# The last 96 features of a float32 gate and up stage: seven products on sums of x for eight on sums of weights

## The chip, the cores and the metric

One core of a Trainium2 chip runs the whole program, in one launch. The metric is device microseconds of that core: the median of the runs shown. One further execution is profiled; it has its own time, and the span of its trace (from the first to the last instruction of the program) is a little shorter than that time. Engines are named as in the profile: PE multiplies matrices, PEld is the loading of its stationary operand, DVE and ACT work on vectors, POOL and SP issue transfers (DMAs), and "PSUM banks" hold PE's results, 128 partitions by 512 float32 each.

## The reference, cut to what matters

One transformer layer in float32 on x of 2 x 2048 tokens by 512: attention over the feature axis, then a feed-forward part whose weights are looked up in a table of 16 values.

```python
x = x + attention(layernorm(x), Wq, Wk, Wv, Wo)
n = layernorm(x)                          # 4096 tokens x 512
gate = n @ lut[gate_idx].T                # 512 -> 1376
up   = n @ lut[up_idx].T                  # 512 -> 1376
x = x + (silu(gate) * up) @ lut[down_idx].T   # 1376 -> 512
```

1376 features are ten blocks of 128 (f = 0 to 9) and a last one of 96 (f = 10). This last block is what the change is about.

## The kernel before

**Stages in order.** Gram matrices of the normalized x (to 77 us), small 512 x 512 products for the attention (to 160), its product with the tokens and the second norm (to 276), gate and up for f = 0 to 9 (to 736.87), gate and up for the last 96 features (to 778.93), and the product with the down weights (to the end, 1052).

**Tiling of gate and up.** The tokens are 8 chunks of 512 (c), taken in four pairs (p). For a feature block f and a pair p a unit (class GateUp) computes four results, gate and up for chunk 2p and for chunk 2p + 1, with the contracted 512 split in two halves of 256. That is a 2 x 2 by 2 x 2 product of blocks, and a unit needs seven block products for it instead of eight, on sums of blocks that are made beforehand: of the weights (S1, S2, S3, S4, by of_both in pair_job, L390, four DVE operations for each f) and of the tokens (T1, T2, T3, T4, by f_sums, in rooms of the pool keep). In the units f = 0 to 9 the weights are stationary (128 x 128, one feature block) and 512 tokens are the moving operand. Each block product is two matmuls of 512 columns into one PSUM bank (mm, L1219). The seven are called a1, c1, a2, c2, b, a3, a4, by the bank they go to; a, c and b are the banks. Products on the same bank follow each other: a2 adds on top of a1 after ACT has copied a1 out, and so on. For f of 2 and above, a second level of the same scheme works on pairs of feature blocks and pairs of p, with banks x, z and w; for it, the operands of the odd p were changed in place (in the products with 21, T4 and 22 the first half stands for a difference).

**Order of the work.** The order on PE, ACT, DVE and SP is written by hand: what the program issues first comes first on its engine. Line.run (L1397) issues the seven products of a unit and, between them, what remains of the unit before: its a4 after the new unit's c1, its Silu (end, L1384) and its product gate x up (out, L1387) still later. between() (L1537) runs after each product: it takes one operation from the list todo, and then fills DVE with steps of the lookup of weights (step, L465; fill, L474) up to a lead over PE that a small clock model (Clock) estimates. The lookup makes all gate, up and down weights from their indices on DVE. Its jobs come in a fixed order; the jobs of the down weights for blocks 0 to 5 store to DRAM (wdd), and wd_load brings these six back into SBUF.

**The last 96 features** (class LastRows, L1452) go another way. Here x is stationary, 128 tokens at a time, and the moving operand is 192 columns, gate and up side by side. ACT copies the looked up weights into one tile side by side (copied, L1465, before the unit f = 9, p = 3), and DVE makes six sums and negatives of them (weights, L1470). For each chunk c, each of four token blocks j takes four matmuls of 192 columns, over the four blocks of 128 of the contracted 512 (products, L1501): 8 x 4 x 4 = 128 matmuls. That is all eight block products; the sums of weights are there only because xs holds some sums of tokens in place of the tokens. Two token blocks share a bank; the banks x, z, w and b take turns. ACT applies Silu to the gate half and DVE multiplies it with the up half (rows, L1516), straight from PSUM, and after the second half of a chunk SP stores 128 x 384 to hrd.

The loop at L1841 goes over the eight chunks and two halves (n = 0 to 15). line.flush (L1443) ends the last unit of f = 9 behind the first four token products. Into the list todo go, in this order: the sums of the weights, wd_load(0) into room sq1 (its load is issued on SP at once, at L1827) with eight DVE sums, the turning back of the norms; wd_load(1) into room a3 when the lookup of blocks 4 and 5 has been issued; sums of the hidden values for the first down unit at n = 8; and the loads of xn_back (ask_for_normed) at n = 12. Then come the units of the down stage (class Down), whose products have 256 columns and go to the banks a, c and b.

Products in LastRows, for one half of a chunk:

```python
for jj in range(2):
    j = 2 * h + jj
    for i, (x, w) in enumerate(pairs):       # four pairs
        nc.tensor.matmul(
            ps[:, jj, :], x[:, j * P : (j + 1) * P], w,
            start=i == 0, stop=i == len(pairs) - 1,
        )
```

Of the kernel before, what the change touches and what calls it, by code (L numbers as in the profile page):

```python
# [51 lines left out]
F32 = mybir.dt.float32  # L52
# [17 lines left out]
def tile_attn_ffn(  # L70
# [303 lines left out]
    def pair_job(f):  # L374
        f0, rows = FT[f]
        n = KB * rows
        made = []

        def dest():
            made.append(wgu.tile([P, 2, KB * P], F32, tag="w", name=f"w_{f}", bufs=4)[:, :, :n])  # L380
            return made[0]

        def after():
            for to, i in ((gw, 0), (uw, 1)):
                to[f] = made[0][:, i, :].rearrange("p (k r) -> p k r", k=KB)
            if f < NFT - 1:
                deferred.append((lambda: f < 3 + ended[0], of_both()))
            yield 0.1

        def of_both():  # L390
            g, u = gw[f], uw[f]
            t = wgu.tile([P, 3, 2, P], F32, tag="s", name=f"s_{f}", bufs=3)
            a11, a12, a21, a22 = g[:, 0:2, :], g[:, 2:4, :], u[:, 0:2, :], u[:, 2:4, :]
            s1, s2, s4 = (t[:, q, :, :rows] for q in range(3))
            for op, d, v, w in (
                (ALU.add, s1, a21, a22), (ALU.subtract, s2, s1, a11),
                (ALU.subtract, a21, a11, a21), (ALU.subtract, s4, a12, s2),
            ):
                nc.vector.tensor_tensor(d, v, w, op)
                yield 0.42  # L400
            gu[f] = {"11": a11, "12": a12, "S3": a21, "22": a22, "S1": s1, "S2": s2, "S4": s4}

        loads = [idx[:, KB * f0 : KB * f0 + n] for idx in (gate_idx, up_idx)]
        return Job(f"w{f}", P, n, loads, dest, after, lambda: f < 4 + ended[0])
# [813 lines left out]

    def mm(ps, pairs, first):  # L1219

        for i, (lhsT, rhs) in enumerate(pairs):
            clock.matmul(rhs.shape[-1])
            nc.tensor.matmul(  # L1223
                ps, lhsT, rhs, start=first and i == 0, stop=i == len(pairs) - 1,
                skip_group_check=not first,
            )
        clock.made(ps)

# [220 lines left out]
            self.last.out()  # L1449
            self.last = None  # L1450

    class LastRows:  # L1452

        TAGS = "xzwb"

        def __init__(self):
            self.w, self.v = (
                wgu.tile([P, 3, 2, P], F32, tag="s", name=f"last_{i}", bufs=3)  # L1460
                .rearrange("p a b c -> p (a b c)").rearrange("p (k r) -> p k r", k=KB)
                for i in range(2)
            )

        def copied(self):  # L1465
            f, r = NFT - 1, LAST
            nc.scalar.copy(self.w[:, :, :r], gw[f])
            nc.scalar.copy(self.w[:, :, r:], uw[f])

        def weights(self):  # L1470
            w, v = self.w, self.v
            u = wgu.tile([P, 2, KB * P], F32, tag="w", name="last_2", bufs=4)
            u = self.u = u.rearrange("p a e -> p (a e)")[:, : 2 * KB * LAST].rearrange(
                "p (k r) -> p k r", k=KB
            )
            minus = nc.vector.tensor_scalar_mul
            return [
                lambda: add(u[:, 0, :], w[:, 2, :], w[:, 3, :]),
                lambda: minus(u[:, 1, :], w[:, 2, :], -1.0),
                lambda: add(v[:, 0:2, :], w[:, 0:2, :], w[:, 2:4, :]),  # L1480
                lambda: minus(v[:, 2:4, :], w[:, 0:2, :], -1.0),
                lambda: add(u[:, 2, :], v[:, 0, :], v[:, 1, :]),
                lambda: minus(u[:, 3, :], v[:, 0, :], -1.0),
            ]

        def pairs(self, c):

            w, v, u, x = self.w, self.v, self.u, xs[c // 2]
            second = c // 2 % 2
            if c % 2 == 0:  # L1490
                one, two = (("11", w[:, 0:2, :]), ("21", w[:, 2:4, :], u[:, 0, :], u[:, 1, :]))
            else:
                one, two = (("T3", v[:, 2:4, :]), ("22", v[:, 0:2, :], u[:, 2, :], u[:, 3, :]))
            t = x[one[0]]
            out = [(t[:, kk, :], one[1][:, kk, :]) for kk in range(2)]
            t = x[two[0]]
            if second:
                return out + [(t[:, 1, :], two[2]), (t[:, 0, :], two[3])]
            return out + [(t[:, kk, :], two[1][:, kk, :]) for kk in range(2)]

        def products(self, c, h, n):  # L1501
            r = 2 * LAST
            ps = psum(self.TAGS[n % 4], f"rows_{c}_{h}")[:, : 2 * r]
            ps = ps.rearrange("p (j r) -> p j r", j=2)
            pairs = self.pairs(c)
            for jj in range(2):
                j = 2 * h + jj
                for i, (x, w) in enumerate(pairs):
                    clock.matmul(r)
                    nc.tensor.matmul(  # L1510
                        ps[:, jj, :], x[:, j * P : (j + 1) * P], w,
                        start=i == 0, stop=i == len(pairs) - 1,
                    )
            return ps

        def rows(self, c, h, ps):  # L1516
            if h == 0:
                t = ffn.tile([P, CH], F32, tag="u2", name=f"hrow_{c}", bufs=2)
                self.h = t[:, : J * LAST].rearrange("p (m j a) -> p m j a", m=M_LAST, j=J)
            g = ffn.tile([P, CH], F32, tag="h0", name=f"grow_{c}_{h}", bufs=2)  # L1520
            g = g[:, : 2 * LAST].rearrange("p (j r) -> p j r", j=2)
            nc.scalar.activation(g, ps[:, :, :LAST], AF.Silu)
            nc.vector.tensor_tensor(  # L1523
                self.h[:, :, 2 * h : 2 * h + 2, :].rearrange("p m j a -> p j m a"),
                g.rearrange("p j (m a) -> p j m a", a=Q),
                ps[:, :, LAST:].rearrange("p j (m a) -> p j m a", a=Q), ALU.mult,
            )
            if h:
                nc.sync.dma_start(hrd[c], self.h)

    sums_of = []
    to_load = []
# [251 lines left out]
    for (f, p), following in zip(units, units[1:] + [(NFT, 0)]):  # L1784
        while f not in gu or f > 1 and p and not all(o.ready(f | 1) for o in seconds):
            clock.dve += step()
        assert p in xs
        if (f, p) == (2, 0):
            sums_of += [(o, f) for o in seconds]
        if 2 < f < NFT - 2 and f % 2 and p == NPR - 1:  # L1790
            sums_of += [(o, f + 1) for o in seconds]
        while f % 2 == 0 and p and sums_of:
            next_sums_left()
        for op in to_load:
            op()
        to_load[:] = loads(*following)
        if (f, p) == (2, 1):
            todo += by_two(in_place)
        if (f, p) == (NFT - 2, NPR - 1):
            while uw.get(NFT - 1) is None:  # L1800
                step()
            last_rows = LastRows()
            last_rows.copied()
        u = GateUp(f, p)
        line.run(u)
        if p == NPR - 1:
            passed[0] = f + 1
        if (f, p) == (0, 3):
            xnp.release()
            x2p = tc.alloc_tile_pool(name="x2p", bufs=1, side="right", reuse_waits="tile")  # L1810
            for g in range(2):
                for o in seconds:
                    ops, last = o.sums(g)
                    todo += [one_by_one(op) for op in ops]
                    in_place.append(last)
# [6 lines left out]
    h = Hidden(0, 0)  # L1822

    def wd_load(q):
        tag, n = (("sq1", 4), ("a3", 2))[q]
        t = room(tag, f"wd_{tag}")
        nc.sync.dma_start(t[:, :n, :], wdd[:, 4 * q : 4 * q + n, :])  # L1827
        wd1.extend(t[:, i, :] for i in range(n))
# [5 lines left out]

        return by_two(down_sums(PARTS[0][2 * q : 2 * q + 2], place))

    while K1 - 4 not in done:
        step()
    todo += by_two(last_rows.weights()) + wd_load(0) + [lambda: [r.turn_back() for r in ln2]]
    n = 0  # L1840
    for c in (0, 4, 2, 6, 1, 5, 3, 7):  # L1841
        for half in range(2):
            ps = last_rows.products(c, half, n)
            if n == 0:
                line.flush()
            last_rows.rows(c, half, ps)
            between()
            n += 1
            if len(wd1) < K1 and (n == 6 or K1 - 2 in done):
                while K1 - 2 not in done:  # L1850
                    step()
                todo += wd_load(1)
            if n == 8:
                todo += by_two(h.sums())
            if n == 12:
                ask_for_normed(0, 0)
                ask_for_normed(0, 1)
    units = [Down(h, 0)]
    for op in todo:
        op()  # L1860
# [95 lines left out]
```

## Time and profile before

| What | Value |
|---|---|
| Median of 3 runs | 1053.54 us (1053.24 to 1054.12) |
| The profiled execution's own time | 1053.92 us |
| Its span | 1052.1 us |
| Mean granted PE clock | 0.999 |
| Gate and up, f = 0 to 9 | 276.00 to 736.87 us |
| Last 96 features | 736.87 to 778.93 us |
| Down stage | 778.93 to 1052 us |

How to read the profile: busy time is the time in which an engine executed something; of PE and PEld the durations of neighbouring instructions overlap, since matmuls are pipelined and a load runs beside the matmul ahead of it. Their ends are modelled; starts are what was recorded. A group of instructions is named by its line in the program, its engine and operation, the tile that it writes, and the tiles that it reads after an arrow. A name such as a_g is bank a of a gate and up unit, a_d that of a down unit, rows the banks of LastRows. "Idle before" is time in which an engine stood still ahead of an instruction, with what ended the wait. "128*128 128x192" means that 128 rows and 128 columns of the array are in use and that the result is 128 by 192.

### The profile page before, as it was taken

To read this page: it belongs to the slowest core of one execution; us is meant where nothing else is said; L and a number is where in the kernel's file an instruction comes from. 1 tells how busy PE (TensorE), PEld (TensorE's weight loads), DVE (VectorE), ACT (ScalarE), POOL (GpSimd) and SP (SyncE) were. 2 spreads that over 40 slices of the span, in tenths; PEclk is the share of its full clock that TensorE was granted. 3 is DMA by queue.
4 is the path that set the end of the run, shared out by engine and by line. 5 is a ranking of instruction groups with operands and counts; after the bars stand their busy time and mean duration, and the time that the engine had idled before them with its cause. 6 is when DMAs were issued, how large, how long until landed. Compare 5 with 4: busy or idle time off the path is not lost.

```text
span 1052.1 us, 11796 instructions
## 1 busy us (share of the span) xinstructions
PE 1044.1 (99%) x3746; PEld 697.3 (66%) x3746; DVE 832.2 (79%) x1558; ACT 397.1 (38%) x769; POOL 107.2 (10%) x160
## 2 busy tenths in 40 slices
PE   9999999999999999999999999999999999999998
PEld 5668888888544444444444444444998888888887
DVE  7888788888898788897898888889668888756644
ACT  4652531566732234434434434444222323211111
POOL 0000000001120210320131032014000000000000
PEclk9999999999999999999999999999999999999999
DMA  8750317268681465885696679569755766566773
GB/s 345 248 167 21 72 23 159 48 158 241 182 229 60 150 209 195 195 230 179 192 198 221 198 175 241 190 174 221 245 159 174 245 202 203 186 198 210 225 220 120
DMA packets 128429, 192.22 MB, mean 183 GB/s; under 512 B 18912, under 2 KB 59104, under 8 KB 127344
## 3 DMA queue, kind: packets, MB, share of 16 engines
q1 hardware_dynamic: 83696, 111.71, 33.4%
q0 software_dynamic: 15776, 39.92, 17.4%
q10 hardware_dynamic: 28896, 39.85, 11.5%
q8 instruction: 29, 0.48, 0.2%
q14 instruction: 32, 0.26, 0.1%
HBM read 110.17 MB, written 81.26 MB: 182 GB/s over the span
## 4 chain that ended last, share of the span: by engine, by line
PE 95%; DVE 2%; DMA 1%; issue 1%; ACT 1%; ACTq 0%; SPq 0%; DVEq 0%
PE a_g L1223 22%; PE a_d L1223 14%; PE y L914 9%; PE c_g L1223 9%; PE c_d L1223 7%; PE gp L542 6%; PE b_d L1223 4%; PE z_g L1223 4%; PE x_g L1223 4%; PE w_g L1223 3%; PE rows L1510 3%; PE b_g L1223 2%; PE ea_t L697 1%; PE ea_s L697 1%; PE ea_p L697 1%; PE ea_m L697 1%
## 5 line engine op out<-in xcount | busy, mean ns | idle before, releaser
L1223 PE MATMUL a_g<-xT_a,s 128*128 128x512 f32 x240 | 113.1, 594 | 0.0
L362 DVE COPY_PREDICATED w<-b_w,w 128x1024 f32<-128x1024 int16 (+1 forms) x77 | 98.6, 1280 | 1.3
L1223 PEld LDWEIGHTS a_g<-xT_a,s 128*128 128x128 f32 x240 | 45.2, 190 | 58.2 <-issue 54.5
L1223 PE MATMUL c_g<-xb,w 128*128 128x512 f32 x160 | 75.3, 593 | 0.9 <-DVE xb L172 0.9
L1223 PE MATMUL a_g<-xb,w 128*128 128x512 f32 x160 | 75.2, 592 | 0.0
L542 PE MATMUL gp<-xn_a 128*128 128x128 f32 (+3 forms) x256 | 69.8, 434 | 0.6 <-DVE xn_a L208 0.5
L350 DVE TENSOR_SCALAR w<-idx_w,lut_x,lut_sb 128x1024 int32<-128x1024 int32 (+1 forms) x88 | 67.9, 794 | 0.2
L1223 PE MATMUL a_d<-dT,hs_a 128*128 128x256 f32 x256 | 65.7, 378 | 0.0
L542 PEld LDWEIGHTS gp<-xn_a 128*128 128x128 f32 x256 | 43.8, 190 | 27.7 <-issue 15.1
L181 ACT COPY p_d<-a_d 128x256 f32<-128x256 f32 x32 | 11.9, 372 | 118.4 <-PE a_d L1223 114.0
L1223 PEld LDWEIGHTS c_g<-xb,w 128*128 128x128 f32 x160 | 30.3, 190 | 39.5 <-issue 36.6
L1223 PEld LDWEIGHTS a_g<-xb,w 128*128 128x128 f32 x160 | 30.4, 190 | 37.9 <-issue 35.2
L1223 PEld LDWEIGHTS a_d<-dT,hs_a 128*128 128x128 f32 x256 | 48.5, 189 | 6.8
L172 DVE TENSOR_TENSOR r<-r,p_d 128x256 f32<-128x256 f32 x64 | 27.1, 423 | 31.7 <-ACT p_d L181 23.4
L362 DVE COPY_PREDICATED wd<-b_wd,wd 128x1024 f32<-128x1024 int16 (+1 forms) x42 | 50.8, 1210 | 0.6
L914 PE MATMUL y<-m,nT 128*128 128x256 f32 x192 | 47.3, 381 | 1.2 <-ACT y L928 0.7
L181 ACT COPY u<-a_g 128x512 f32<-128x512 f32 x40 | 23.4, 586 | 58.1 <-PE a_g L1223 58.0
L172 DVE TENSOR_TENSOR r<-r,a_d 128x256 f32<-128x256 f32 x64 | 26.7, 418 | 20.4 <-PE a_d L1223 20.4
L1510 PEld LDWEIGHTS rows<-last,xb 128*128 128x128 f32 x256 | 41.6, 190 | 1.0 <-DVE hrow L1523 0.5
L1510 PE MATMUL rows<-last,xb 128*128 128x192 f32 x256 | 42.0, 326 | 0.2 <-DVE hrow L1523 0.2
L172 DVE TENSOR_TENSOR c<-a_g,p 128x512 f32<-128x512 f32 x40 | 27.6, 689 | 18.1 <-PE a_g L1223 17.0
L914 PEld LDWEIGHTS y<-m,nT 128*128 128x128 f32 x192 | 36.2, 190 | 7.2 <-ACT y L928 1.5
(368 smaller groups left out, 2228.8 us busy)
## 6 DMA issues: line engine op xcount, KB each, us to landing
hd<-h SPq DMA_DIRECT2D x80, 256.0 KB, 3.5
h<-hd SPq DMA_DIRECT2D x40, 512.0 KB, 6.1
nl<-nd SPq DMA_DIRECT2D x32, 256.0 KB, 5.7
xnd<-xn_f SPq DMA_DIRECT2D x16, 512.0 KB, 5.6
fl<-xnd POOLq DMA_DIRECT2D x32, 256.0 KB, 6.4
xn_back<-xnd SPq DMA_DIRECT2D x32, 256.0 KB, 3.7
rd<-r SPq DMA_DIRECT2D x32, 256.0 KB, 2.6
r<-rd SPq DMA_DIRECT2D x32, 256.0 KB, 3.5
```

The source lines that it names most:

```text
L172: nc.vector.tensor_tensor(dest, a, b, op)
L181: nc.scalar.copy(dest, a)
L350: vec.tensor_scalar(dest.bitcast(I32), idx, lut_x[:rows, k : k + 1], lut_i[:rows, at : at + 1], ALU.bitwise_and, ALU.bitwise_xor,)
L362: vec.copy_predicated(dest, masks[level - 1], t)
L542: nc.tensor.matmul(gp[b][i][:, i * P :], xn[:, i, j % 2, :], xn[:, i:, j % 2, :], start=c % CPB == 0 and j == 0, stop=c % CPB == CPB - 1 a ...
L697: nc.tensor.matmul(ps[:, m, :], self.a[a][:, k, m * P : (m + 1) * P], self.b[b][:, k, :], start=first and m == k == 0, stop=k == 1, skip_g ...
L914: nc.tensor.matmul(to, self.n[a][:, k, self.s, :], self.m[b][:, k, :], start=first and k == 0, stop=k == 1, skip_group_check=not first,)
L1223: nc.tensor.matmul(ps, lhsT, rhs, start=first and i == 0, stop=i == len(pairs) - 1, skip_group_check=not first,)
L1510: nc.tensor.matmul(ps[:, jj, :], x[:, j * P : (j + 1) * P], w, start=i == 0, stop=i == len(pairs) - 1,)
```

## The change

LastRows and its loop go. The last 96 features are computed by four units of a new class LastUnit, a GateUp whose seven block products have x, or sums of x, stationary: 128 tokens by 128 of the contracted axis. The moving operand is 96 columns of a weight block or of a sum of weight blocks. The four token blocks of a chunk lie side by side in one bank (4 x 96 columns). A block product is eight matmuls of 96 columns (four token blocks by two halves of 256). The four results of a unit go through GateUp's own steps (copies from PSUM by ACT, sums by DVE, Silu), on 384 columns. The products gate x up go to hrd as before, one chunk at a time.

Other edits: the four sums of weights are now made for f = 10 too (pair_job); last_weights makes, for the odd p, three more tiles with a negative and a sum in place of the two halves (six DVE operations of 96 columns, issued before the unit f = 9, p = 3). The ACT copies side by side and the six sums of LastRows go. mm takes an optional place in the bank. wd_load uses the rooms x7 and x5 in place of sq1 and a3, and is called after the first and second unit; for that the units go in the order p = 3, 0, 1, 2. The other entries of todo move to the third unit, and the last unit's a4, Silu and product are issued after what is left in todo. The units use the banks a, b and c.

The diff, cut to its core:

```diff
@@ pair_job.after
-            if f < NFT - 1:
-                deferred.append((lambda: f < 3 + ended[0], of_both()))
+            deferred.append((lambda: f < 3 + ended[0], of_both()))
@@ mm
-        for i, (lhsT, rhs) in enumerate(pairs):
+        for i, (lhsT, rhs, *at) in enumerate(pairs):
             clock.matmul(rhs.shape[-1])
             nc.tensor.matmul(
-                ps, lhsT, rhs, start=first and i == 0, stop=i == len(pairs) - 1,
-                skip_group_check=not first,
+                ps[:, at[0]] if at else ps, lhsT, rhs, start=first and i == 0,
+                stop=i == len(pairs) - 1 or pairs[i + 1][2:] != (*at,),
+                skip_group_check=not first or at not in ([], [0]),
             )
-    class LastRows:
...
+    class LastUnit(GateUp):
+        def __init__(self, p):
+            super().__init__(NFT - 1, p)
+            self.rows, self.role = P, None
+
+        def pairs(self, a, b):
+            w, x = (last_w if self.p % 2 and a in last_w else gu[self.f])[a], xs[self.p][b]
+            return [
+                (x[:, kk, j * P : (j + 1) * P], w[:, kk, :LAST], j)
+                for j in range(J) for kk in range(2)
+            ]
...
+        def product(self, h, v, tag, c):
+            t = super().temp(tag)[:, : J * LAST].rearrange("p (m j a) -> p m j a", m=M_LAST, j=J)
+            h, v = (u.rearrange("p j (m a) -> p j m a", a=Q) for u in (h, v))
+            tensor(t.rearrange("p m j a -> p j m a"), h, v, ALU.mult)
+            nc.sync.dma_start(hrd[c], t)
+
+        def first(self):
+            self.product(self.h0, self.u2, "p1", 2 * self.p)
+
+        def out(self):
+            self.product(self.h1, self.c22, "y", 2 * self.p + 1)
+
+    def last_weights():
+        t = wgu.tile([P, 3, 2, P], F32, tag="s", name="last_w", bufs=3)
+        for q, a in enumerate(("12", "22", "S4")):
+            w, v = gu[NFT - 1][a], t[:, q, :, :LAST]
+            nc.vector.tensor_scalar_mul(v[:, 0, :], w[:, 0, :], -1.0)
+            add(v[:, 1, :], w[:, 0, :], w[:, 1, :])
+            last_w[a] = v
@@ before the unit f = 9, p = 3
-            while uw.get(NFT - 1) is None:
+            while NFT - 1 not in gu:
                 step()
-            last_rows = LastRows()
-            last_rows.copied()
+            last_weights()
@@ wd_load
-        tag, n = (("sq1", 4), ("a3", 2))[q]
+        tag, n = (("x7", 4), ("x5", 2))[q]
@@ the stage
-    for c in (0, 4, 2, 6, 1, 5, 3, 7):
...
+    order = (3, 0, 1, 2)
+    for n, p in enumerate(order):
+        u = LastUnit(p)
+        line.run(u, final=n == NPR - 1)
+        if n == 0:
+            while K1 - 4 not in done:
+                step()
+            todo += [lambda: [r.turn_back() for r in ln2]] + wd_load(0)
+        if n == 1:
+            while K1 - 2 not in done:
+                step()
+            todo += wd_load(1)
+        if n == 2:
+            ask_for_normed(0, 0)
+            ask_for_normed(0, 1)
+            todo += by_two(h.sums())
+    u.a4()
+    u.end()
+    u.out()
+    line.last = None
     units = [Down(h, 0)]
```

More of the change, by code (lines that the diff above doesn't have):

```diff
@@ L1450, in flush @@
             self.last = None
-    class LastRows:
[L1456 to L1476, printed above, removed]
-            return [
[L1478 to L1483, printed above, removed]
-            ]
[L1486 to L1529, printed above, removed]
@@ new lines, in tile_attn_ffn, with side_by_side, view, temp @@
+    class LastUnit(GateUp):
[4 more added lines that the diff above has]
+            w, x = (last_w if self.p % 2 and a in last_w else gu[self.f])[a], xs[self.p][b]
+            return [
+                (x[:, kk, j * P : (j + 1) * P], w[:, kk, :LAST], j)
+                for j in range(J) for kk in range(2)
+            ]
+        def side_by_side(self, t):
+            return t[:, : J * LAST].rearrange("p (j r) -> p j r", j=J)
+        def view(self, tag):
+            return self.side_by_side(super().view(tag))
+        def temp(self, tag, bufs=1):
+            return self.side_by_side(super().temp(tag, bufs))
+        def product(self, h, v, tag, c):
[7 more added lines that the diff above has]
+            self.product(self.h1, self.c22, "y", 2 * self.p + 1)
@@ L1531, in tile_attn_ffn @@
+    last_w = {}
+    def last_weights():
[5 more added lines that the diff above has]
+            last_w[a] = v
     sums_of = []
@@ L1835, in wd_load @@
         return by_two(down_sums(PARTS[0][2 * q : 2 * q + 2], place))
[L1837 to L1840, printed above, removed]
-    for c in (0, 4, 2, 6, 1, 5, 3, 7):
[L1842 to L1857, printed above, removed]
+    order = (3, 0, 1, 2)
[18 more added lines that the diff above has]
+    line.last = None
     units = [Down(h, 0)]
```

## The prediction

> **What bounds the kernel now.** I read the page's busy table first, then the stage of the last features by a table of busy time, then that stage's line, then single weight loads in the timeline. In the first fence the columns are busy time, share of the span and instructions. In the second they are the length of a stretch (of the gate and up stage, then of the last features) and the busy time of PE, PEld, DVE, ACT and POOL in it.
>
> ```profile
> PE 1044.1 (99%) x3746; PEld 697.3 (66%) x3746; DVE 832.2 (79%) x1558; ACT 397.1 (38%) x769; POOL 107.2 (10%) x160
> ```
> ```profile
> 276.00:736.87 460.87, 459.57 (x1069) 201.76 (x1068) 394.73 (x594) 191.62 (x324) 92.26 (x127) 1.00 0.69 192
> 736.87:778.93 42.06, 41.88 (x258) 41.58 (x257) 23.97 (x64) 7.56 (x19) 0.55 (x1) 1.00 0.60 191
> ```
>
> PE is never idle for long, and its granted clock is 1.00 in the stage, so what the change does to PE's time there goes into the span one for one. In the 42.06 us of the last features the weight loads (PEld) are busy 41.58, in the main stage only 201.76 of 460.87. DVE and ACT have 18 and 34 us free in these 42. Now the stage's matmuls and loads: count, then duration in ns (least, median, most), then first and last start.
>
> ```profile
> L1510 PEld LDWEIGHTS rows<-last,xb x256: 186/190/190, 736.4 to 778.6; 128*128 128x128 f32 x128
> L1510 PE MATMUL rows<-last,xb x256: 326/326/430, 736.9 to 778.8; 128*128 128x192 f32 x128
> ```
>
> The code has 128 matmuls there and the profile 256: each float32 product goes as two passes, each with its own weight load. The durations (326 and 190) overlap, so I don't add them up; I take distances between starts. Eight 192-column passes in a row, without a wait, show as one group of 1.46 us at 774.70: (1.46 - 0.326)/7 = 0.162 us. Four 256-column passes at 782.81 take 1.03 us, (1.03 - 0.379)/3 = 0.217. So a pass costs 0.833 ns a column and 2.5 ns more, and 96 columns alone would cost 82.5 ns.
>
> That holds only while the next weights are in the array by then. The evidence on a load comes from a place where one was late (start, length, engine, line, operation, count, and in brackets the idle time before it). It is the last product before the stage:
>
> ```profile
> 735.05 0.30 PEld L1223 LDWEIGHTS a_g<-xT_sq,s 128*128 128x128 f32 x2 [0.65 <-ACT u L181]
> 735.07 1.96 PE L1223 MATMUL a_g<-xT_sq,s 128*128 128x512 f32 x4
> 735.59 0.19 PEld L1223 LDWEIGHTS a_g<-xT_sq,s 128*128 128x128 f32 x1 [0.24 <-issue]
> ```
>
> The first load starts at 735.05. The second starts 0.30 - 0.19 = 0.11 us later and the third at 735.59. The last of the four passes starts at 735.07 + 1.96 - 0.59 = 736.44; at 429 ns a pass (0.833 x 512 + 2.5) the second started at 735.585 and the first really streamed from 735.157. So the array took the weights **106 ns after the load began**, although the load's row says 190, and **the next load began only when this pass began** (735.16): one set of weights ahead, no more. The third shows the same: it starts with the second pass. The 128-column transposes are the shortest passes that come in a row:
>
> ```profile
> 50.68 0.69 PEld L605 LDWEIGHTS gt<-ident,g 128*128 128x128 f32 x6
> 50.79 0.82 PE L605 MATMUL gt<-ident,g 128*128 128x128 f32 x6
> ```
>
> Passes: (0.82 - 0.27)/5 = 0.110 us. Loads: (0.69 - 0.14)/5 = 0.110 us. At 128 columns the two costs meet; below that the load must be the longer one.
>
> **The change part by part.**
>
> *Products.* Removed: 128 matmuls of 192 columns, 256 passes x 162.5 ns = 41.6 us. The stage took 42.06; the other 0.46 is a wait of its own (DVE stood 4.3 us at 747.4 for the landing of wd_sq, and PE lost 0.35 and 0.11 at 755). Added: 4 units x 7 products x 8 matmuls = 224 of 96 columns, each again with a stationary block of 128 columns that is used once: 448 passes and 448 loads. By columns the change saves an eighth (21,504 for 24,576), but the loads grow from 256 to 448. At a load-bound distance of 106 + 2.5 = 108.5 to the 110 of the transposes I take 109 ns: 448 x 0.109 = 48.8 us. Change: 48.8 - 42.06 = **+6.8 us**. Bounds: 82.5 ns, if the loads hid (37.0 us, -5.1), and 112 ns, the largest distance between neighbouring loads of 128-column products in the first stage (50.2 us, +8.1). I take 109 since both near rows say so. PEld's 190 ns as a distance (85 us, +43) is excluded by the transposes.
>
> Two rules of the Trainium skill pull apart here. "TensorE: Matmul & The Clock Gate", section "Back-to-back issue gap", gives N/2.4 + 2.5 ns for a lone matmul and warns that this leaves the weight load out at small N; taken at its word (two clocks a column here), a pass is 82.5 ns and the change gains 5.1 us, which the row at 735.05 speaks against. "Perfetto Trace Analysis", section "Identifying the Most-Contended Engine", judges TensorE's headroom by the busy share of LDWEIGHTS; by that the stage of before, at 99%, is at its load limit with 162 ns a load, and 448 loads would take 72.8 us, +30.7. The rows say neither: the load takes 106 ns of those 162.
>
> *Evictions and products on ACT and DVE.* Removed: 16 Silu of 331 ns, 16 multiplications of 350, six sums of weights (2.1 us on DVE) and two copies (1.0 us on ACT, at 730.6). Added per unit: 3 copies and 2 Silu of 384 columns on ACT (between 372 ns for 256 and 631 for 512, about 0.5), and 4 DVE operations of about 0.55. That is 10 us on ACT and 9 us on DVE in 48.8: hidden. The waits in a unit have cover: a product onto bank a follows the copy (or sum) of the one before by two other products, 3.5 us (one, 1.75 us, in the first and the last unit), for an operation of 0.5. At the end b stands between a3 and a4 and covers the sum.
>
> *Weights, before the stage.* Four sums of 192 columns (354 ns each) and six of 96 columns (at most 0.25 to 0.35) move into the last features but one, at most 3.2 us of DVE, where it is busy 39.0 of 45 us (690 to 735). The lookup of the down weights yields; two to four of its steps move past the stage's start, and they are due only after the second unit. If that cover were gone, PE would lose up to 3.2 us; I take nothing.
>
> *SP's queue.* wd_load(0) now goes into room x7, which the first unit reads until c2, and stands on SP behind the first unit's store. That store waits for a DVE product after b: about 736.9 + 6 x 1.74 + 1.5 = 748.9. Landing took 9.6 us for wd_sq (1 MB, in traffic) and 3.9 for wd_a (half): 752.8 to 758.5. DVE waits there, and behind it stand about 5 us of sums up to the second unit's a3 sum, 763.5 at the latest; the a4 that needs it is due at 736.9 + 15 x 1.74 = 763.0. Cost 0 to 0.5 us; I take 0. wd_load(1) and the four loads of xn_back move too, with over 8 us to spare each.
>
> *Sum.* The profiled execution took 1053.92 us, 1.8 more than its span; 1053.92 + 6.8 = 1060.7. The median of the runs is 0.4 lower: **1060.3 us**.
>
> **The rivals.**
>
> 1. *Loads bind, and nothing else does* (the forecast): 1060.3. For: the late load, the transposes. Against: no row has fewer than 128 columns.
> 2. *The stream binds* (the other side): at 96 columns the loads are pulled two ahead, or use less than 82.5 ns when another load has just ended. Stage 37.0 us: 1053.5 - 5.1 = 1048.4. It decides from the point where a load needs less than the pass. Against: worked out in the same way, every late load of this trace shows 105 or 106 ns, and no load starts before the pass ahead of it.
> 3. *Load and stream meet half way*: about 94 ns a pass, 448 x 0.094 = 42.1: no change, 1053.5. No row speaks for it.
> 4. *Loads bind and a wait comes on top*: 112 ns a pass and the up to 0.5 us of SP's queue, or a first unit that waits for ACT behind the main stage's last Silu. 50.2 + 1.5: 1063.2.
> 5. *It doesn't do what it says*: one pass for a product or a load that serves two matmuls. The order of the built program has 224 matmuls of 96 columns, each with another block of x, so I give that nothing.
>
> **How the numbers follow.** Forecast 82 in 100, rival 4: 11, rival 2: 4, rival 3: 3. Range: 108 ns and no wait give +6.3, rounded down by a little for gains elsewhere; 112 ns and 1.5 us of waits give +9.6. So 1058.5 to 1063.2, which leaves out rivals 2 and 3 and some of 4. About 0.2% (2.1 us) is what a measurement of this kernel can tell from no change: slower 93 in 100, the same 3, faster 4.
>
> **What would show it right or wrong.** In the changed kernel's trace the 96-column passes should start 108 to 112 ns apart, with each load starting at the pass before it, and PE's stage should last 48 to 50 us from the last 512-column pass to the first of the down stage. Distances near 83 show rival 2; distances of 109 with holes of over 0.3 us between units show rival 4, and the timeline names who was waited for (ACT's copy, DVE's sum or the landing of wd_x). Before and after the stage the two traces should agree within 0.5 us. The forecast is wrong if the loads come closer than 105 ns anywhere in the stage.

## The result and the profile after

| | before | after |
|---|---|---|
| Median of the runs (lowest to highest), us | 1053.83 (1053.24 to 1054.15), 4 runs | 1063.15 (1063.01 to 1063.33), 4 runs |
| Profiled execution, its span, us | 1053.92, 1052.1 | 1063.33, 1061.5 |
| To the end of f = 9, us | 736.87 | 738.26 |
| Last 96 features, us | 42.05 | 50.00 |
| Down stage, us | 273.2 | 273.3 |

After / before is 1.0089, with a 95% interval of 1.0072 to 1.0107. In the profiled executions the 9.41 us more are 7.95 in the stage, 1.39 ahead of it and 0.03 in the down stage; the last 0.04 lie outside the span. The busy table of after comes first. Then come its last three stages, each cut slightly wide: start and end, length, busy time of PE, PEld, DVE, ACT and POOL with their instructions, the clock, the DMA share and GB/s.

```profile
PE 1052.1 (99%) x3938; PEld 705.7 (66%) x3938; DVE 835.5 (79%) x1562; ACT 400.8 (38%) x771; POOL 106.1 (10%) x160
```
```profile
276.00:738.26 462.26, 459.65 (x1068) 201.73 (x1067) 395.34 (x603) 191.95 (x323) 90.55 (x126) 1.00 0.69 191
738.26:788.38 50.11, 50.11 (x450) 50.11 (x449) 26.38 (x59) 10.68 (x22) 1.09 (x2) 1.00 0.51 161
788.38:1061.50 273.12, 269.68 (x1249) 236.54 (x1247) 190.44 (x454) 60.34 (x131) 1.59 (x3) 1.00 0.64 201
```

The down stage of before, in the same columns:

```profile
778.93:1052.00 273.07, 269.75 (x1249) 236.64 (x1248) 190.28 (x454) 60.19 (x131) 1.59 (x3) 1.00 0.64 200
```

PE gained 192 passes (3938 for 3746), the 448 that came less the 256 that went. In the stage PE has no idle time, the clock is 1.00, and DVE and ACT have 24 and 39 us free. The other stage that grew is the main one: PE's busy time in it is the same (459.65 for 459.57), so those 1.4 us are a wait.

**In the stage**, one group of its line, with count, durations (least, median, most) and first and last start:

```profile
L1222 PEld LDWEIGHTS a_g<-s,xT_a x96: 192/192/192, 754.2 to 784.5; 128*128 128x128 f32 x96
L1222 PE MATMUL a_g<-s,xT_a x96: 275/275/275, 754.3 to 784.6; 128*128 128x96 f32 x96
```

The start of the stage in the timelines of PE and PEld:

```profile
738.26 1.92 PE L1222 MATMUL a_g<-w,xb 128*128 128x96 f32 x16
740.02 1.17 PE L1222 MATMUL c_g<-w,xb 128*128 128x96 f32 x9
```
```profile
738.27 1.75 PEld L1222 LDWEIGHTS a_g<-w,xb 128*128 128x128 f32 x15 [0.24 <-issue]
739.94 1.20 PEld L1222 LDWEIGHTS c_g<-w,xb 128*128 128x128 f32 x10
```

The durations overlap again, so distances are taken. Passes: (1.17 - 0.275)/8 = 0.112 us. Loads: (1.20 - 0.192)/9 = 0.112. All passes but the first stand 111 or 112 ns apart, and no load of the stage comes closer to the one before it than 110; over the stage it is 50.00/448 = 111.6 a pass, and 111.7 in the steady rows. A 96-column stream alone would need 82.5. Each load starts 29 ns after the recorded start of the pass ahead of it: one load ahead, no more. No pass in the stage waits for another engine.

**Ahead of the stage**, DVE and PE near 715 us in after. The operation h<-a_g,y on DVE, called h below, is the sum that reads bank a before PE's next product goes into it:

```profile
716.22 1.53 DVE L350 TENSOR_SCALAR wd<-idx_wd,lut_x,lut_sb 128x1024 int32<-128x1024 int32 x2 [2.98 <-DMA wdd<-wd]
...
718.45 0.69 DVE L172 TENSOR_TENSOR h<-a_g,y 128x512 f32<-128x512 f32 x1
```
```profile
719.19 1.55 PE L1222 MATMUL a_g<-xb,w 128*128 128x512 f32 x3 [1.32 <-DVE h L172]
```

and the same places in before:

```profile
713.47 1.54 DVE L350 TENSOR_SCALAR wd<-idx_wd,lut_x,lut_sb 128x1024 int32<-128x1024 int32 x2 [0.73 <-DMA wdd<-wd]
...
717.01 0.69 DVE L172 TENSOR_TENSOR h<-a_g,y 128x512 f32<-128x512 f32 x1
```
```profile
717.91 1.88 PE L1223 MATMUL a_g<-xb,w 128*128 128x512 f32 x4
```

DVE starts the lookup of the down weights of blocks 4 and 5 in the tile of those of blocks 2 and 3, which has one buffer. So it must wait until the store of the latter (wdd) has landed. In before that wait is 0.73 us, h is done at 717.70, and PE takes it at 717.91 without idle time. In after the wait is 2.98, h is done at 719.14, and PE takes it at 719.19. By distances between passes PE lost 1.49 us there, and 0.10 behind it. The store itself, on SP's queue, first in before, then in after:

```profile
708.18 0.32 SPq L423 DMA_DIRECT2D wdd<-wd  x1
708.75 0.32 SPq L1250 DMA_DIRECT2D hd<-h  x1
```
```profile
708.57 0.32 SPq L1250 DMA_DIRECT2D hd<-h  x1
708.94 0.43 SPq L422 DMA_DIRECT2D wdd<-wd  x1
```

The two stores have changed places. The wdd store is issued 0.76 us later and takes 7.2 us to land where it took 5.2: it lands at 716.13 for 713.37. In after h starts 2.32 us behind that landing, and PE 0.05 us behind the end of h.

### The profile page after: what moved, and what is told of

It is laid out like the page before. It is cut to its first block, busy times and chain, and to the rows that moved or that the text cites. A ratio compares the mean times of both kernels' runs of the same rounds, so it can differ in the third digit from the quotient of the medians.

```text
span 1061.5 us, 12193 instructions
## 1 busy us (share of the span) xinstructions
PE 1052.1 (99%) x3938; PEld 705.7 (66%) x3938; DVE 835.5 (79%) x1562; ACT 400.8 (38%) x771; POOL 106.1 (10%) x160
## 5 line engine op out<-in xcount | busy, mean ns | idle before, releaser
L181 ACT COPY u<-a_g 128x512 f32<-128x512 f32 (+1 forms) x44 | 25.4, 576 | 68.7 <-PE a_g L1222 68.6
L172 DVE TENSOR_TENSOR c<-a_g,p 128x512 f32<-128x512 f32 (+1 forms) x44 | 29.8, 677 | 22.1 <-PE a_g L1222 20.7
L181 ACT COPY p<-c_g 128x512 f32<-128x512 f32 (+1 forms) x44 | 25.3, 576 | 46.5 <-PE c_g L1222 45.3
L172 DVE TENSOR_TENSOR u<-c_g,u 128x512 f32<-128x512 f32 (+1 forms) x44 | 29.6, 673 | 14.3 <-PE c_g L1222 12.5
```

The costliest lines, as they stand in the source:

```text
L172: nc.vector.tensor_tensor(dest, a, b, op)
L181: nc.scalar.copy(dest, a)
```

## The experiments

Theory: the load of 128 stationary columns sets the distance of the passes, whatever the moving columns are; and the four new sums of f = 10, made among the lookup's steps, push the wdd store behind hd<-h on SP, which costs PE 1.4 us. Rivals: the distance follows the moving columns plus a fixed cost, or a cost that each pass has whatever its size; and for the 1.4 us, that they belong to the new stage or to chance.

### The stage: which operand sets the distance

**64 moving columns for 96** (x unchanged):

```diff
-                (x[:, kk, j * P : (j + 1) * P], w[:, kk, :LAST], j)
+                (x[:, kk, j * P : j * P + 128], w[:, kk, :64], j)
...
```

> The changed kernel with 64 of the 96 moving columns in the last stage (it leaves out the last 32 of each 96 features; the middle 32 are written twice in their place). Theory, the load of 128 stationary columns sets the distance of the passes: nothing changes, 448 passes at 111.7 ns, stage 50.0 us, about 1063 us. Rival, each pass costs its columns and a fixed 29 ns more (111.7 - 82.5): 55.8 + 29.2 = 85.0 ns, stage 38.1 us, about 1051 us.

**128 moving columns** (weights of another block):

```diff
-            w, x = (last_w if self.p % 2 and a in last_w else gu[self.f])[a], xs[self.p][b]
+            w, x = gu[self.f - 1][a], xs[self.p][b]
...
-                (x[:, kk, j * P : (j + 1) * P], w[:, kk, :LAST], j)
+                (x[:, kk, j * P : (j + 1) * P], w[:, kk, :], j)
...
```

> The changed kernel with 128 moving columns instead of 96 (it takes the weights of feature block 9 in place of the last block's, so the last 96 features are not computed). Theory, loads set the distance: a pass of 109.2 ns still fits under the load's 111.7, stage 50.0 us, about 1063 us. Rival, columns and a fixed 29 ns: 138.4 ns, stage 62.0 us, about 1075 us.

One execution each: 1062.72 and 1063.17 us, beside 1053.76 of before. Two products from the middle of the stage, at 64 moving columns and then at 128:

```profile
748.36 1.95 PE L1222 MATMUL a_g<-w,xb 128*128 128x64 f32 x16
750.15 1.95 PE L1222 MATMUL c_g<-w,xb 128*128 128x64 f32 x16
```
```profile
748.79 1.95 PE L1222 MATMUL a_g<-w,xb 128*128 128x128 f32 x16
750.58 1.95 PE L1222 MATMUL c_g<-w,xb 128*128 128x128 f32 x16
```

In both the second product starts 1.79 us after the first, and within a product a pass takes (1.95 - 0.275)/15 = 111.7 ns, at 64 columns as at 128; the stages last 49.97 and 50.02 us. Twice the moving columns are free here. That excludes any law in which the moving columns count at these sizes. A cost that each pass has whatever its size is left, and the next two runs exclude it.

**64 stationary columns for 128**, with 96 and with 64 moving. Half of each token block goes uncomputed:

```diff
-            self.rows, self.role = P, None
+            self.rows, self.role = 64, None
...
-                (x[:, kk, j * P : (j + 1) * P], w[:, kk, :LAST], j)
+                (x[:, kk, j * P : j * P + 64], w[:, kk, :96], j)
...
```

> The changed kernel with 64 of the 128 stationary columns (it leaves out half of the tokens of each block in the last stage; the other half's results are stored twice). Theory, loads set the distance and take 0.83 ns a column: a load of about 59 ns hides under the pass, 82.5 ns a pass, stage 37.0 us, about 1050 us. Rivals, a fixed distance or a cost of columns and 29 ns, both blind to the stationary side: 111.7 ns, stage 50.0 us, about 1063 us.

> The changed kernel with 64 stationary and 64 moving columns (it leaves out half of the tokens and a third of the features of the last stage). Theory: the longer of a load of about 59 ns (53 and a handover of 5) and a pass of 55.8: 59 ns, stage 26.4 us, about 1039.5 us, if DVE and the landing of the down weights keep up. Rival, columns and a fixed 29 ns: 85 ns, stage 38.1 us, about 1051 us.

One execution each: 1056.13 and 1055.85 us. Rows of the first, then of the second:

```profile
752.47 1.48 PE L1222 MATMUL b_g<-w,xb 128*64 128x96 f32 x16
753.79 1.48 PE L1222 MATMUL a_g<-s,xT_a 128*64 128x96 f32 x16
...
761.88 1.66 PE L1222 MATMUL a_g<-s,xb 128*64 128x96 f32 x16 [3.97 <-DVE c L172]
```
```profile
747.75 1.10 PE L1222 MATMUL a_g<-s,xT_a 128*64 128x64 f32 x16
748.69 1.10 PE L1222 MATMUL c_g<-w,xT_a 128*64 128x64 f32 x16
```

Per pass: (753.79 - 752.47)/16 = 82.5 ns, the stream's own price for 96 columns, and (1.10 - 0.222)/15 = 58.5 ns (58.3 is the mean of the 346 passes that nothing disturbed). So the theory of the pass distance holds: with half the load the stream binds at 96 columns, and the load again at 64. The totals missed. Both expectations priced the stage by the passes alone, at 37.0 and 26.4 us (the second on the condition that DVE and the landing of the down weights keep up); the stages lasted 43.14 and 42.11. The faster stage ran into the next limit, which the idle time at 761.88 names. It is a sum on DVE, and DVE in that kernel stood for SP's queue:

```profile
757.23 0.42 DVE L172 TENSOR_TENSOR dT<-wd_x 128x256 f32<-128x256 f32 x1 [7.50 <-DMA wd_x<-wdd]
```

That is the landing of wd_load(0) that the prediction had priced at 0 to 0.5 us. After the wait came a stretch at half clock, told of below. In the second of the two there are waits of 5.1, 3.1 and 2.0 us.

**96 stationary and 64 moving columns**, to test the law at a size not used for finding it:

```diff
-            self.rows, self.role = P, None
+            self.rows, self.role = 96, None
...
-                (x[:, kk, j * P : (j + 1) * P], w[:, kk, :LAST], j)
+                (x[:, kk, j * P : j * P + 96], w[:, kk, :64], j)
...
```

> The changed kernel with 96 stationary and 64 moving columns (it leaves out a quarter of the tokens and a third of the features of the last stage). Theory, a distance is the longer of 0.833 ns a moving column and 2.5, and of 0.833 ns a stationary column and 5.1: the load, 85.1 ns, 448 passes in 38.1 us, to which a wait for the down weights' landing may come (4 us in the kernel with 64 stationary columns). Rival, a load of fewer than 128 columns hides altogether: 55.8 ns.

```profile
753.19 1.52 PE L1222 MATMUL b_g<-w,xb 128*96 128x64 f32 x16
754.55 1.52 PE L1222 MATMUL a_g<-s,xT_a 128*96 128x64 f32 x16
```

(754.55 - 753.19)/16 = 85 ns: the size fits to 0.1. The stage's length does not, 49.6 us in a run of 1063.97: besides 448 x 85 = 38.1 us of work it had two waits (1.7 and 2.8 us longer than a pass) and 93 passes at half clock, 75 ns more each (7.0 us), which the expectation didn't have.

All sizes together, at full clock:

| stationary | moving | ns a pass | where |
|---|---|---|---|
| 128 | 192 | 162.5 | before |
| 128 | 64, 96, 128 | 111.7 | experiments and after |
| 96 | 64 | 85 | experiment |
| 64 | 96 | 82.5 | experiment |
| 64 | 64 | 58.3 | experiment |

One rule gives all of them to 0.2 ns: the greater of 0.833 ns x moving columns + 2.5 and 0.833 ns x stationary columns + 5.1. The 5.1 was fitted to the rows with 128 and with 64 stationary columns; the row with 96 was the test. The busy row of a load (192, 165 and 138 ns at 128, 96 and 64 columns, with the moving columns of the load-bound rows) is no distance: it is 80 ns longer than the distances of 111.7, 85 and 58.3. The Trainium skill, "TensorE: Matmul & The Clock Gate", section "LDWEIGHTS (loading the stationary operand)", gives the time of a load in ns as its columns over 1.2: 106.7 at 128. The distances here are 5.0 ns longer.

### The 1.4 us ahead of the stage

**The sums of f = 10 taken out of the lookup**, and issued just before the unit f = 9, p = 3 instead:

```diff
-            deferred.append((lambda: f < 3 + ended[0], of_both()))
+            if f < NFT - 1:
+                deferred.append((lambda: f < 3 + ended[0], of_both()))
+            else:
+                last_sums.append(of_both())
...
+            for _ in last_sums[0]:
+                pass
             last_weights()
```

> The changed kernel, with the four sums of the last block's weights made together just before the unit f = 9, p = 3, and not among the lookup's steps; the steps and SP's stores then stand up to there as in the kernel before. Theory, the sums cost by moving the store of the looked up down weights behind another store on SP, whose later landing DVE waits for: PE's hole of 1.5 and 0.1 us at 719 is gone, the stage starts near 736.9 instead of 738.3, about 1061.6 us. Rival, the sums' own 1.4 us of DVE work is what PE lost: the hole only moves to about 730, 1062.8 us or more.

Median 1062.40 us of 5 runs (1061.80 to 1063.13), ratio to before 1.0076 (1.0062 to 1.0089). On SP the store stands first again, at 708.21, and DVE's wait is 0.89 us. PE's loss is 0.50 where it was 1.59: DVE is still 0.6 us behind its place in before, and the margin there was 0.2. So the theory's 1061.6 was met in part. What is left needs no work of the sums: the store, issued as early as in before, landed 0.59 us later (713.96).

```profile
714.05 1.53 DVE L350 TENSOR_SCALAR wd<-idx_wd,lut_x,lut_sb 128x1024 int32<-128x1024 int32 x2 [0.89 <-DMA wdd<-wd]
...
717.59 0.69 DVE L172 TENSOR_TENSOR h<-a_g,y 128x512 f32<-128x512 f32 x1
```

**Before with the four sums, and nothing else of the change:**

```diff
-            if f < NFT - 1:
-                deferred.append((lambda: f < 3 + ended[0], of_both()))
+            deferred.append((lambda: f < 3 + ended[0], of_both()))
...
```

> The kernel before with the four sums for the last block added alone, at the place where the changed kernel has them (nothing reads them; the third is written to its own tile and not in place). Theory, the store's landing: a hole of 0.6 to 1.6 us at about 719 in the main stage, 1054.4 to 1055.4 us. Rival, the hole comes from the changed last stage or from the ACT copies that it drops: no hole, 1053.8 us.

The order on SP turned round, the store was issued at 709.07, and DVE waited 2.89 us:

```profile
715.62 1.53 DVE L350 TENSOR_SCALAR wd<-idx_wd,lut_x,lut_sb 128x1024 int32<-128x1024 int32 x2 [2.89 <-DMA wdd<-wd]
...
717.85 0.69 DVE L172 TENSOR_TENSOR h<-a_g,y 128x512 f32<-128x512 f32 x1
```
```profile
718.59 1.98 PE L1223 MATMUL a_g<-xb,w 128*128 128x512 f32 x4 [0.57 <-DVE h L172]
```

PE lost 0.84 us there, in a kernel whose last stage is the old one. So the sums alone make the wait, not the new stage. Nor is it DVE time that their own work takes just ahead of h, since DVE stands idle there for 2.89 us. The time, 1054.79 us of 11 runs (1053.61 to 1055.55), is a ratio of 1.0004 (0.9995 to 1.0013), no difference that can be measured; in its trace the 0.45 us that PE lost inside the old stage are gone, which hides half of the 0.84.

**The store issued by ACT**, meant to take it from behind hd<-h:

```diff
-                nc.sync.dma_start(wdd[:rows, i : i + k, :], made[0])
+                nc.scalar.dma_start(wdd[:rows, i : i + k, :], made[0])
```

> The changed kernel, with the three stores of the looked up down weights issued by ACT and not by SP, so that none stands behind a store of hidden values; the sums stay where they are. Theory, the store's landing: DVE's wait for it near 713 falls from 3.0 us to about 1 and PE's hole at 719 to below 0.3 us, about 1061.8 us. Rival, the sums' own DVE work: hole and time as in the changed kernel, 1063.1 us.

1063.24 us of 4 runs, ratio 1.0084 (1.0070 to 1.0098), not the 1061.8 of the theory. In the program's order the store stands behind a Silu on ACT, and that waited for DVE:

```profile
709.56 0.63 ACT L1341 ACTIVATE h<-h 128x512 f32<-128x512 f32 x1 [1.05 <-DVE h L172]
709.57 0.33 ACTq L422 DMA_DIRECT2D wdd<-wd  x1
```

It went out 0.63 us later than in after, so the experiment didn't test what it was for. It shows only that leaving SP is not enough.

**The store issued right behind the lookup's last step**, ahead of hd<-h, with the sums where the change put them:

```diff
+                if level == 4:
+                    self.at_once()
...
-        def after():
+        def at_once():
             if i < K1:
                 nc.sync.dma_start(wdd[:rows, i : i + k, :], made[0])
+
+        def after():
...
```

> The changed kernel, with the store of looked up down weights issued straight behind the last step of its lookup and not with the step after it; on SP it then stands ahead of the store of hidden values that it stands behind in the changed kernel. The sums stay. Theory, the place on SP: the store is issued near 708.0 and not 708.9, DVE's wait for its landing near 713 falls from 2.7 to 3.0 us to about 1, PE's hole at 719 from 0.7 to 1.6 us to below 0.5, about 1062.2 us. Rival, the landing is late for the traffic and not for the place: DVE waits 2 us or more again, 1063.2 us.

1061.95 us of 5 runs (1061.62 to 1063.27), ratio to before 1.0073 (1.0060 to 1.0087). SP, DVE and PE in it:

```profile
708.49 0.32 SPq L425 DMA_DIRECT2D wdd<-wd  x1
709.05 0.52 SPq L1257 DMA_DIRECT2D hd<-h  x1
```
```profile
715.26 1.53 DVE L351 TENSOR_SCALAR wd<-idx_wd,lut_x,lut_sb 128x1024 int32<-128x1024 int32 x2 [1.80 <-DMA wdd<-wd]
...
717.48 0.69 DVE L172 TENSOR_TENSOR h<-a_g,y 128x512 f32<-128x512 f32 x1
```
```profile
718.23 1.98 PE L1229 MATMUL a_g<-xb,w 128*128 128x512 f32 x4
```

No idle time stands at PE's product any more: of the 1.59 us 0.10 is left, with the sums still among the lookup's steps. About 1.0 of that is the store's doing, which landed at 715.16 for 716.13. The other 0.5 is luck: in this trace PE had lost 0.6 us at 514.5, as in some of the others and not in after, and so came to this place 0.5 us later. The stage starts 0.96 us earlier than in after (737.30), and the median is 1.2 us lower; the intervals of the two ratios overlap, so the time only agrees with the trace. DVE still waited 1.80 us, nearer to the rival's 2 than to the theory's 1.

**From the landing to PE.** Nine traces have the sums among the lookup's steps: those of after, of the five kernels with other columns, of before with the sums, of the store issued by ACT, and of this kernel. In eight of them h starts 2.32 us after the store has landed, and in one 2.44; in all but this kernel's PE starts some 0.05 us after h ends. So what PE loses follows from when the store lands and from how far PE itself has come. The loss differs from trace to trace: 0.70, 1.05, 1.28, 1.32 and 0.88 us in the five kernels with other columns (in the order of this text), which are the same as after up to the new stage, and 1.59 in after, the most of the nine. The four runs of after lie within 0.3 us; why the others differ from it is not shown.

What stays open is why the landing took longer. The store in second place on SP took 6.3 to 7.2 us to land in seven kernels. In first place it took 5.2, 5.3 and 5.8 us in three, but 6.7 here. The place on SP explains when it is issued, and not the whole of how long it takes. A second buffer for the tile was not tried.

### The 0.46 us that the old stage lost

**Before, with wd_load(0) and its sums later in the list todo**, so that DVE doesn't stand for the landing of wd_sq:

```diff
-    todo += by_two(last_rows.weights()) + wd_load(0) + [lambda: [r.turn_back() for r in ln2]]
+    todo += by_two(last_rows.weights()) + [lambda: [r.turn_back() for r in ln2]]
+    todo += [lambda: None] + wd_load(0)
```

> The kernel before with the sums of the down weights taken from the list two places later, after the norms are turned back and one empty place; their load is issued two places later, too. Theory, the 0.46 us that the last stage loses in the kernel before is DVE's wait for that load: the stage shortens from 42.06 to about 41.6 us, 1053.4 us. Rival, the wait only moves, since the load is issued later as well: 1053.8 us or up to 0.5 more.

The load itself was not issued later: it stands at 741.98 in both, so only the sums moved, and the rival of the expectation couldn't arise. The stage lasted 41.60 us, and PE lost nothing in it. The time is 1053.97 us of 11 runs (1053.16 to 1056.31), ratio 1.0000 (0.9991 to 1.0009): too small to measure, and a loss of 0.82 us at 515 in the profiled execution outweighs it there. Since the stage of before with the sums alone lasted 41.60 as well, the 0.46 is a matter of small shifts and not a fixed part of the old stage.

No kernel of this study is faster than before.

## Why the prediction was off by 2.9 us

| Step | Predicted, us | Measured, us | From |
|---|---|---|---|
| 448 passes | 48.8 (109 ns) | 50.0 (111.7 ns) | trace of after |
| What they replace | 42.06 | 42.05 | trace of before |
| Weights, before the stage | 0 | 1.4 | wait at 719.19, less 0.2 of small gains |
| SP's queue, ACT and DVE in the stage | 0 | 0 | no idle time in it |
| Sum | +6.8 | +9.4 | profiled executions |

That is 2.6 us. The other 0.2 to 0.3 come from the step to the median, which was taken to be 0.4 us below the profiled execution and lay 0.2 below it in after.

*Products.* The sign, the mechanism and the count were right, and 64, 96 and 128 moving columns at one distance show that the load binds. The term was mis-sized: "I take 109 since both near rows say so" failed by 2.7 ns a pass, 448 x 2.7 = 1.2 us. Both near rows were short: a load that came late once, and a row of six transpose passes. The bound of 112, from neighbouring loads of 128-column products, was the price. The runs bear out neither of the two readings of the Trainium skill's pages in the prediction: the moving columns alone (82.5 ns) are what a pass costs at 64 stationary columns and not at 128, and a load's busy row (192 ns) is never a distance.

*Weights, before the stage.* "I take nothing" failed, and it is the larger error. The prediction saw that up to 3.2 us of DVE work moved and that the lookup yields. But it followed only the lookup's results, which are due late, and not the other thing that the lookup's last step issues: a store on SP, for whose landing DVE itself waits before the next lookup. The sum h, which PE needs, stood behind that wait. With the sums alone in before the wait is there (0.84 us of PE); with the store in first place again PE lost 0.50 or 0.10.

*SP's queue.* The landing of wd_load(0) was put at 752.8 to 758.5; DVE began on it at 758.83. The sum behind it that PE needs ended at 763.45, and PE began the a4 at 765.0, so 1.6 us of cover were left. Part of that cover is the slower pass: at 1.74 us a product the prediction had the a4 due at 763.0. With 64 stationary columns the cover is gone and PE stood for 4.2 us.

*Evictions and products on ACT and DVE.* Hidden, as said: PE never waits in the stage.

*Before and after the stage within 0.5 us.* True after it (0.03), false before it (1.39).

*Rivals.* The stream didn't bind, nor did load and stream meet half way. The sum came out as rival 4's, 112 ns and a wait of 1.4 us, and its price of 1063.2, also the upper end of the range, is the time. Its distance was right; its wait was right in size only, by luck. The places that it named for it, SP's queue of wd_load(0) and ACT in the first unit, cost nothing; the wait stood 19 us ahead of the stage.

The old stage's 0.46 us were counted as gone with it, and in the trace of after they are. The variant of before without them is no faster by measurement.

## What to carry to other kernels

A pass of a float32 product with a stationary block used once cost the greater of stream and load here, 0.833 ns x moving + 2.5 and 0.833 ns x stationary + 5.1. Seven products for eight with the moving columns halved are 448 passes for 256, and short passes run into the load's price. By that rule, as an estimate that no run tested, 448 passes of 111.7 ns equal 256 passes of 232 columns: at 128 stationary columns the exchange gains only when the halved columns are above some 116. Take the price of a load-bound row from a long row of loads, not from a single late one. When work moves on an engine that has little idle time, follow what its displaced steps issue, DMAs above all, to whoever waits for their landing.

## What the hardware showed beyond that

After longer waits of PE the granted clock fell to half. This is the stage with 96 stationary columns by stretches (columns as in the first section):

```profile
736.90:760.20 23.30, 21.89 (x244) 20.94 (x242) 14.38 (x37) 5.45 (x13) 2.29 (x4) 1.00 0.68 213
760.20:772.60 12.40, 9.73 (x112) 9.59 (x112) 5.93 (x14) 2.69 (x6) 0.00 (x0) 1.00 0.35 116
772.60:787.90 15.30, 15.24 (x97) 15.24 (x97) 6.82 (x21) 1.40 (x4) 0.00 (x0) 0.51 0.40 115
```

Two starts 1.75 us apart (at 760.29) left the clock at 1.00; 2.88 us (at 772.66) brought it to 0.51 until beyond the end of the stage, though PE was never idle in that stretch. There a pass took 160 ns, 2 x 0.833 x 96 with nothing added. With 64 stationary columns a distance of 2.0 us left the passes after it at full speed, and those of 3.1, 4.2 and 5.1 us were followed by 3.4, 3.4 and 5.7 us at half clock. So in these three kernels a wait of about 3 us cost its own length and some us more.

The Trainium skill, "TensorE: Matmul & The Clock Gate", section "What's actually happening", puts the fall after at least one idle window of some 3.4 us and the return after at least one busy window of the same length. The two returns after 3.4 us agree with it. The falls after 2.88 and 3.1 us are earlier, and the 15 us in which the clock stayed at half with PE busy are more than four such windows.

Also unexpected: 128-column passes in a long row stand 111.7 ns apart, and in a row of six transpose passes 110. What the last 5 ns of a load are was not found.
